# An adaLN block of gated linear attention and an FP4 feed-forward: modulation loads moved to other slots, and the last rows' down products in two column halves

## The chip, the cores and the metric

The kernel runs on one core of one Trainium2 chip. The metric is the device time of one execution in microseconds; the median of several runs is compared. The profile is one further execution, taken by the hardware profiler.

## What is computed

The input x has 2 batches of 4096 rows of 512. Six modulation rows per batch come from a small product. The first half of the block is a gated scan, the second a feed-forward whose operands are quantized blockwise to FP4 and back.

```python
mod = (_silu(L0_c) @ L0_wmod).reshape(2, 6, 1, -1)
sa, ca, ga, sb, cb, gb = (mod[:, i] for i in range(6))
ga, gb = (sign(g) * max(abs(g), 0.25) for g in (ga, gb))
h = layernorm(x) * (1 + ca) + sa
x = x + ga * attn(h)      # q, kv, a = rmsnorm(h) @ W; y = scan(sigmoid(a), kv); q * y
h = layernorm(x) * (1 + cb) + sb
x = x + gb * ffn(h)       # fp4(silu(fp4(h) @ wg) * (fp4(h) @ wu)) @ fp4(wd)
```

`ffn` has an inner width of 1408. Products that have to be nearly as exact as float32 are made as three passes over pairs of 16-bit parts (high x high, high x low, low x high); `PASSES` at line 419 lists them.

## The kernel before, in words

**Two stages.** The 8192 rows are 64 tiles of 128 rows (`NT`). Stage one makes the attention for 16 blocks of 512 rows (4 tiles each) and stores x plus the gated result to `out`. It also quantizes the feed-forward's weights on the side. Stage two takes the 64 tiles one after another through the feed-forward.

**Stage one, slots.** The loop at line 850 goes over slots 4 to 66 (the opening at line 717 holds slots 0 to 3 and the preparation of weights). Slot `i * 4 + e` makes the products of block `i` for output columns `e` of 128: `mix` (line 421), 3 parts (gate, value, query) x 4 chunks x 3 passes = 36 products of 128x512, each part in a PSUM bank; even and odd slots use different banks. Within the same slot stand the steps of other work, in a written order:

- tile `g = slot + 4` of the next block: `norm_hi` on ACT, `norm_lo` (line 403 on DVE, then `norm_turn`, line 409: the DMA transpose of this tile into the block's `xT`). The fourth of these transposes belongs to slot `4i + 3`, and the first product of slot `4i + 4` needs it.
- the previous slot's products: sigmoid (line 442), scan on DVE (448), read-out (459), a copy that splits halves (`yh`, 466), its DMA transpose `yt` (471); two slots on the joined copy (477), the residual add on POOL (485) and the store (490).
- moments and centring of the tiles after that; the load of x for tile `g + 3` (line 360).
- units of weight work: slots 5 to 21 load two weight pieces each for their maxima (`plan`), then come `collect`, `spread` and `finish` (lines 527 to 540: the maxima go through DRAM to all partitions), then one piece a slot is quantized, its transpose at line 553 or 576.

The whole stage stands in `tc.manual_schedule`, so each engine has the instructions of its queue in the order in which the Python code makes them. SP issues all loads and transposes in one queue; POOL issues the stores. In a slot SP has, in this order: the loads of the coming weight pieces (503 or 509), the load of x (360), the transpose `xT` (409), the transpose `yt` (471), the transpose of a quantized weight piece, and last the modulation loads.

**Modulations.** Rows 0 to 2 are made in the opening. Rows 3, 4 and 5 are made later: `load_mod` (line 224) brings `wmod` in quarters of 256 KB, one at the end of each of slots 5 to 16; `mod_rows` (line 238) makes the products after slot 19's own; at the end of slot 20 `mod_store` turns them to rows (lines 255 to 258 and 267) and POOL stores them to DRAM (line 270). `mod_load` (line 281, its issue in the profile at 283) loads one such row, spread over 128 partitions (256 KB): two of them at the end of slot 36 (`mods_for(0)`), and `mod_gb`, the gate of the feed-forward's output, at the end of slot 38.

```python
    MODS = 19
            rows = mod_rows(3, 4, 5) if slot == MODS else None
            if MODS - 14 <= slot < MODS - 2:
                m, k = divmod(slot - MODS + 14, KC)
                load_mod(3 + m, k, k + 1)
            if slot == NS // 2 + KC + 2:
                gbs[0] = mod_load(5, 0, "mod_gb")
```

**Stage two.** For each tile: `products` (line 947, 72 products), `silu`, `gated`, `quant_h`, and two tiles later `down` (line 994): 33 products of 128x512 into one PSUM tile (11 chunks x 3 passes). `finish` scales the result (line 1012) and adds it to `out` by an accumulating store from POOL (1018). The last tile is different: its x was loaded to `last_x1`, and `finish` scales, adds (1023) and stores (1024, on SP) two halves of 256 columns one after the other, both after the one sum of 33 products.

Of the kernel before, what the change touches and what calls it, by code (L numbers as in the profile page):

```python
# [8 lines left out]
F32 = mybir.dt.float32  # L9
# [4 lines left out]
ALU = mybir.AluOpType  # L14
# [4 lines left out]
P = 128  # L19
D = 512  # L20
KC = D // P
B = 2
N = 4096
# [8 lines left out]
NT = B * N // P  # L32
# [12 lines left out]
def tile_adaln_block(  # L45
# [13 lines left out]
    V, A, G, T, S = nc.vector, nc.scalar, nc.gpsimd, nc.tensor, nc.sync  # L59
# [16 lines left out]
    def side(shape):  # L76
        return pst.tile(list(shape), F32, name="sd", tag="sd")
# [18 lines left out]
    ring = None  # L96
# [318 lines left out]
    def new_xT():  # L415
        return apool.tile([P, 2 * KC, TB], F16, name="xT", tag="xT", bufs=2)
# [140 lines left out]
    def wd_chunk(wp, k):  # L557
        j = k * P // 512
        n0, n1 = CHUNKS[j]
        return 2 * (n0 // P) + wp * ((n1 - n0) // P) + k - n0 // P  # L560
# [34 lines left out]
    def load_units(items):  # L595
        got = []
        for kind, arg in items:
            if kind in ("max", "rows"):
                got.append((kind, arg, load_rows(arg[2], arg[0])))
            elif kind in ("maxd", "down"):  # L600
                got.append((kind, arg, load_down(*arg)))
            else:
                got.append((kind, arg, None))
        return got
# [7 lines left out]
    qx, x1s, xst, gbs = {}, {}, {}, {}  # L612
# [223 lines left out]
    def step(gen, n=1):  # L836
        for _ in range(n):
            if gen is not None:
                next(gen, None)
# [1 line left out]
    units, coming = [], []  # L841
    rows = None
    NS = NBLK * KC
    MODS = 19
    plan = [[]] * (KC + 1) + plan
    order = tc.manual_schedule(engines={V.engine, A.engine, G.engine, S.engine, T.engine})
    with order:
        xT, nxT = new_xT(), new_xT()
        gate, joining = opening(xT, nxT)
        for slot in range(KC, NS + 3):  # L850
            i, e = divmod(slot, KC)
            if e == 0 and slot < NS:
                xT = nxT
                nxT = new_xT() if i + 1 < NBLK else None
            units, coming = coming, load_units(plan[slot]) if slot < len(plan) else []
            g = slot + KC
            if g + 3 < NT:
                norm_load(g + 3)
            cur = None
            if slot < NS:  # L860
                got = []
                step(mix(i, xT, e, got), 3)
                cur = got[0]
            late = rows
            rows = mod_rows(3, 4, 5) if slot == MODS else None
            if slot == KC:
                gate = gates(*gate)
            if len(joining) == 2 or slot >= NS + 2:
                store(*residual(*joined(*joining.pop(0))))
            if g < NT:  # L870
                norm_hi(g)
            if gate is not None:
                gate = scan(*gate)
                carry_on(*gate)
            if g + 2 < NT:
                norm_moments(g + 2)
            if gate is not None:
                gate = read_out(*gate)
            if g < NT:
                norm_lo(g, nxT)  # L880
            if gate is not None:
                joining.append(turned(*halves(*gate)))
            if g + 2 < NT:
                norm_stats(g + 2)
            for u in units:
                u.advance(1)
            if g + 1 < NT:
                norm_center(g + 1)
            for u in units:
                u.advance(2)  # L890
                u.advance(3)
            if cur is not None:
                cur = gates(*cur)
            if g + 1 < NT:
                norm_shift(g + 1)
                norm_square(g + 1)
            for u in units:
                u.advance(4)
            coming = [Unit(*c_) for c_ in coming]
            for u in coming:  # L900
                u.advance(0)
            if g + 1 < NT:
                norm_gain(g + 1, G)
            for u in units:
                u.advance(5)
                u.advance(6)
            assert all(u.step == 7 for u in units)
            if MODS - 14 <= slot < MODS - 2:
                m, k = divmod(slot - MODS + 14, KC)
                load_mod(3 + m, k, k + 1)  # L910
            if late is not None:
                mod_store(*late)
            if slot == KC + 1:
                ca[1] = mod_load(1, 1, "mod_c1")
                sa[1] = mod_load(0, 1, "mod_s1")
            if slot == NS // 2 + KC:
                mods_for(0)
            if slot == NS // 2 + KC + 2:
                gbs[0] = mod_load(5, 0, "mod_gb")
            if slot in (NS - 6, NS - 5):  # L920
                for n in range(2):
                    n += 2 * (slot - NS + 6)
                    x1s[n] = load_x1(n)
            if NS - 5 <= slot < NS - 1:
                n = slot - NS + 5
                xst[n] = stats_x(x1s[n])
                if n in (1, 2):
                    run(quant_x(n - 1, x1s.pop(n - 1), xst.pop(n - 1)))
            gate = cur
    tc.no_sync_barrier()  # L930
    wgT, wuT, wdT = wts["wgT"], wts["wuT"], wts["wdT"]
# [3 lines left out]
    ring = ctx.enter_context(tc.tile_pool(name="ring", bufs=2))  # L935
# [49 lines left out]
        S.dma_start_transpose(hT, flat(hl))  # L985
        qh[i] = hT, u

    def down(i):
        hT, u = qh.pop(i)
        pd = side((P, D))  # L990
        n = 0
        for k in range(IC):
            for hp, wp in PASSES:
                T.matmul(  # L994
                    pd,
                    hT[:, hp * IC + k, :],
                    wdT[:, wd_chunk(wp, k), :],
                    start=n == 0,
                    stop=n == 3 * IC - 1,
                )  # L1000
                n += 1
        return i, pd, u

    def finish(i, pd, u):
        b, t0 = divmod(i * P, N)
        if b not in gbs:
            t = ring.tile([P, D], F32, name="mod_gb1", tag="mod_gb1", bufs=1)
            S.dma_start(t, modd[5][b : b + 1, :].to_broadcast([P, D]))
            gbs[b] = t
        o = ring.tile([P, D], F32, name="o", tag="o", bufs=3)  # L1010
        def scaled(d):
            V.scalar_tensor_tensor(  # L1012
                out=o[:, d], in0=pd[:, d], scalar=u, in1=gbs[b][:, d], op0=ALU.mult, op1=ALU.mult
            )

        if i < NT - 1:
            scaled(slice(0, D))
            G.dma_start(out[b, t0 : t0 + P, :], o, accum_op=ALU.add)  # L1018
            return
        for d0 in range(0, D, D // 2):  # L1020
            d = slice(d0, d0 + D // 2)
            scaled(d)
            V.tensor_tensor(o[:, d], o[:, d], last_x1[:, d], ALU.add)
            S.dma_start(out[b, t0 : t0 + P, d], o[:, d])

    LAG, LEAD = 2, 2
    qh = {}
# [4 lines left out]
    with tc.manual_schedule(engines={V.engine, A.engine, G.engine, S.engine, T.engine}):  # L1032
        h = None
        ended = []
        for i in range(NT):
            last = i == NT - 1
            work_i = products(i)
            downs = [] if i == NT - 2 else [i - LAG - 1, i - LAG] if last else [i - LAG]
            ending, ended = ended, [down(d) for d in downs if d >= 0]
            x = None  # L1040
            if i + LEAD < NT:
                x = quant_x(i + LEAD, x1s.pop(i + LEAD), xst.pop(i + LEAD))
            if i + LEAD + 2 < NT:
                x1s[i + LEAD + 2] = load_x1(i + LEAD + 2)
            step(x, 2)
            step(h)
            step(h)
            step(h, 2)
            sl = silu(0, *work_i)
            step(x)  # L1050
            if i + LEAD + 1 < NT and i > 0:
                xst[i + LEAD + 1] = stats_x(x1s[i + LEAD + 1])
            step(x)
            gated(0, sl, *work_i)
            step(x)
            sl = silu(1, *work_i)
            step(x)
            for e in ending:
                finish(*e)
            step(x, 4)  # L1060
            gated(1, sl, *work_i)
            gated(2, silu(2, *work_i), *work_i)
            h = quant_h(i, work_i[2])
            step(h, 3)
        step(h, 2)
        last_x1 = load_x1(NT - 1)
        finish(*ended.pop(0))
        step(h, 3)
        ended.append(down(NT - 2))
        finish(*ended.pop(0))  # L1070
        ended.append(down(NT - 1))
        for e in ended:
            finish(*e)


_TC = dict(schedule_with_timeline_sim=True)
# [45 lines left out]
```

## Time and profile before

| | |
|---|---|
| runs, median (lowest to highest) | 1910.6 us (1909.87 to 1911.59) |
| the profiled execution's own time | 1910.41 us |
| its span in the profile | 1908.3 us |
| granted TensorE clock | 0.999 |
| stage one / stage two, from the chain of waits | up to 534.3 us / after it |
| DMA share in 61.8 to 124.7, 124.7 to 187.0, 187.0 to 347.7 us | 0.93, 0.82, 0.80 |
| DMA share in 534.3 to 1875.0 us | 0.39 |
| SP's loads of `wmod`: count, median to landing | 24, 4.7 us |
| SP's `xT` and `yt` transposes: count, median to landing | 64 and 64, 3.5 and 3.2 us |

A row of the timeline has the start, the duration (of the whole group where several are merged), the engine, the line of the kernel, the operation, output<-input, the shape and the count; in brackets stands the idle time of that engine before it and what released it. PE is TensorE's products, PEld its weight loads, which run beside products. Ends of products are modelled, so a row's duration covers about 0.16 us more than the time to the next start. SPq rows are DMA issues: the duration is that of the issue, and the landing is told apart from it. The chain of waits follows the work that ended last back to what released each step.

### The profile page before, as it was taken

Reading aid. Unit: us, or ns where it says so; the run is one execution under the profiler, and the core shown is the slowest. Engines: PE = TensorE matmul, PEld = TensorE weight load, DVE = VectorE, ACT = ScalarE, POOL = GpSimd, SP = SyncE. Lnnn points to the kernel's source line nnn. Section 1 sums busy time; section 2 is a strip of 40 time slices with the busy share of each in tenths; the row PEclk is TensorE's granted clock in tenths of the full one; section 3 lists DMA queues with packets and bytes.
Section 4 is the critical chain, followed back from the end, with each engine's and each line's share of the span. In section 5 each row is a group of like instructions: output and inputs, shape, how many; then the busy total and the mean of one; then the engine's idle time right before and its main releaser. Section 6 shows DMA issues by size and latency. Waiting matters only on the chain.

```text
span 1908.3 us, 25838 instructions
## 1 busy us (share of the span) xinstructions
PE 1893.5 (99%) x9342; PEld 901.9 (47%) x9342; DVE 1603.3 (84%) x2670; ACT 999.1 (52%) x1702; POOL 407.7 (21%) x596
## 2 busy tenths in 40 slices
PE   8999999999999999999999999999999999999998
PEld 5444444444444444444444444444444444444444
DVE  7888799999869988888888888888888888888865
ACT  6555577777655544445444444445444544444432
POOL 5545566666421100000000000000000000000000
PEclk9999999999999999999999999999999999999999
DMA  6787679888533533433344334443344334433433
GB/s 222 196 240 214 155 197 201 218 199 202 134 86 64 96 64 68 80 75 64 64 79 80 64 64 86 77 74 67 69 80 75 64 64 80 80 64 64 70 62 59
DMA packets 469185, 203.26 MB, mean 107 GB/s; under 512 B 426247, under 2 KB 427527, under 8 KB 469057
## 3 DMA queue, kind: packets, MB, share of 16 engines
q1 hardware_dynamic: 454608, 168.09, 40.9%
q0 software_dynamic: 14448, 33.52, 9.1%
q8 instruction: 73, 1.20, 0.3%
q14 instruction: 56, 0.45, 0.1%
HBM read 62.86 MB, written 33.58 MB: 51 GB/s over the span
## 4 chain that ended last, share of the span: by engine, by line
PE 92%; DVE 4%; DMA 2%; ACT 1%; issue 1%; POOL 0%; SPq 0%; ACTq 0%; DVEq 0%
PE mm L947 47%; PE sd L994 24%; PE mm L430 20%; DVE ld L176 1%; PE sd L230 0%; DMA yt<-yh 0%; DMA xr<-in_L_attn_x_dram 0%; DVE hl L403 0%; DVE ld L170 0%; ACT y L477 0%; DVE y L448 0%; DMA xT<-hl 0%; DMA scratch<-in_L_wmod_dram 0%; DVE scratch L334 0%; DVE y L459 0%
## 5 line engine op out<-in xcount | busy, mean ns | idle before, releaser
L947 PEld LDWEIGHTS <-x2T 128*128 128x128 f16 x4608 | 450.9, 98 | 469.0 <-issue 0.8
L430 PE MATMUL mm<-xT,wqT 128*128 128x512 f16 (+1 forms) x2412 | 499.0, 370 | 3.2 <-ACT cy L454 1.6
L947 PE MATMUL mm<-wuT,x2T 128*128 128x512 f16 (+1 forms) x2304 | 487.7, 361 | 0.5 <-DVE hid L967 0.5
L947 PE MATMUL mm<-wgT,x2T 128*128 128x512 f16 (+1 forms) x2304 | 487.7, 361 | 0.0
L994 PE MATMUL sd<-wdT,hT 128*128 128x512 f16 x2112 | 465.8, 379 | 0.0
L430 PEld LDWEIGHTS <-wqT 128*128 128x128 f16 x2412 | 229.4, 98 | 271.7 <-issue 4.4
L994 PEld LDWEIGHTS <-hT 128*128 128x128 f16 x2112 | 206.6, 98 | 242.7
L962 ACT ACTIVATE silu<-mm,u 128x512 f32<-128x512 f32 (+1 forms) x192 | 124.7, 650 | 284.9 <-PE mm L947 281.1
L967 DVE SCALAR_TENSOR_TENSOR hid<-mm,u,silu 128x512 f32<-128x512 f32 (+1 forms) x192 | 128.6, 673 | 138.8 <-PE mm L947 130.2
L635 POOL TENSOR_SCALAR rstd<-vs 128x1 f32<-128x1 f32 x64 | 14.9, 232 | 989.1 <-ACT sq L633 989.1
L144 ACT ACTIVATE u<-ud,rms 128x1 f32<-128x1 f32 x64 | 18.9, 295 | 278.8 <-DVE rms L140 278.8
L121 ACT ACTIVATE sle<-sl 128x512 f16<-128x512 f32 (+2 forms) x162 | 146.9, 907 | 0.0
L114 ACT ACTIVATE she<-sh 128x1408 bf16<-128x1408 bf16 (+1 forms) x128 | 128.3, 1002 | 4.1
L1018 POOL DMA_DIRECT2D out_dram<-o x63 | 55.5, 881 | 271.4 <-DVE o L1012 267.6
L466 ACT COPY yh<-y 128x1024 uint16<-128x1024 uint16 x64 | 66.9, 1045 | 88.4 <-DVE y L459 80.5
L123 DVE SCALAR_TENSOR_TENSOR xn<-hid,xn 128x1408 f32<-128x1408 f32 x64 | 103.6, 1619 | 3.7 <-ACT hid L117 3.7
L107 DVE TENSOR_TENSOR xn<-hid,inv 128x1408 f32<-128x1408 f32 x64 | 104.0, 1625 | 2.2
L126 DVE SCALAR_TENSOR_TENSOR hhl<-hid,xn 128x1408 f16<-128x1408 f32 x64 | 104.0, 1625 | 2.2
L148 DVE TENSOR_REDUCE amh<-hid 128x88 f32<-128x1408 f32 x64 | 103.7, 1620 | 2.2
L117 ACT ACTIVATE hid<-xn 128x1408 f32<-128x1408 f32 x64 | 88.1, 1377 | 30.9 <-DVE xn L107 30.9
L123 DVE SCALAR_TENSOR_TENSOR xn<-ld,xn 128x512 f32<-128x512 f32 (+1 forms) x98 | 67.1, 684 | 29.5 <-ACT ld L117 29.3
L485 POOL TENSOR_TENSOR xr<-xr,y 128x512 f32<-128x512 f32 x64 | 81.9, 1279 | 18.7 <-ACT y L477 14.8
(129 smaller groups left out, 1913.2 us busy)
## 6 DMA issues: line engine op xcount, KB each, us to landing
ld<-out_dram SPq DMA_DIRECT2D x65, 256.0 KB, 2.9
xr<-in_L_attn_x_dram SPq DMA_DIRECT2D x64, 256.0 KB, 3.7
out_dram<-xr POOLq DMA_DIRECT2D x64, 256.0 KB, 3.7
out_dram<-o POOLq DMA_DIRECT2D x63, 256.0 KB, 3.9
scratch<-in_L_wmod_dram SPq DMA_DIRECT2D x24, 256.0 KB, 4.7
ld<-in_L_ffn_w_gate_dram SPq DMA_DIRECT2D x22, 256.0 KB, 3.4
ld<-in_L_ffn_w_up_dram SPq DMA_DIRECT2D x22, 256.0 KB, 3.7
ld<-in_L_ffn_w_down_dram SPq DMA_DIRECT2D x16, 256.0 KB, 3.3
```

The costliest lines, as they stand in the source:

```text
L107: V.tensor_tensor(blocks(xn), blocks(src), spread(inv, nb), ALU.mult)
L114: A.activation(blocks(she), spread(sh, nb), AF.Copy, scale=WPEAK)
L117: A.activation(a, xn, AF.Abs, scale=MAGIC)
L121: A.activation(blocks(sle), spread(sl, nb), AF.Copy, scale=WPEAK)
L123: V.scalar_tensor_tensor(out=xn, in0=a, scalar=FLOOR, in1=xn, op0=ALU.max, op1=ALU.add)
L126: V.scalar_tensor_tensor(out=nq, in0=a, scalar=FLOOR, in1=xn, op0=ALU.max, op1=ALU.subtract)
L148: V.tensor_reduce(am, src.rearrange("p (b k) -> p b k", k=QB), AX.X, ALU.max, apply_absolute_value=True)
L430: T.matmul(pp[:, t : t + width], wqT[e][:, wp, k, part, :], xT[:, xp * KC + k, t : t + width], start=n == 0, stop=n == 3 * KC - 1,)
L947: T.matmul(pp[:, : n1 - n0], x2T[:, xp * KC + k, :], wt[:, wp * KC + k, n0:n1], start=n == 0, stop=n == 3 * KC - 1,)
L962: A.activation(sl[:, :w], pairs[j][0][:, :w], AF.Silu, scale=u[:, 0:1])
L967: V.scalar_tensor_tensor(out=hid[:, n0:n1], in0=pairs[j][1][:, : n1 - n0], scalar=u[:, 1:2], in1=sl[:, : n1 - n0], op0=ALU.mult, op1=ALU.mult,
L994: T.matmul(pd, hT[:, hp * IC + k, :], wdT[:, wd_chunk(wp, k), :], start=n == 0, stop=n == 3 * IC - 1,)
```

## The change

The products of rows 3 to 5 move from slot 19 to slot 22. The twelve quarter loads keep their order but stand at the ends of those slots from 5 to 20 that aren't 6, 10, 14 or 18. `mod_gb`'s load moves from the end of slot 38 to the end of slot 40. The last tile's down products are made by `last_down`, as two sums of 33 products of 256 columns in two banks of `products`; each half is scaled, added and stored by itself. The order on the other engines is otherwise the same; in stage two, instructions differ in the last tile alone.

```diff
-    MODS = 19
+    MODS = 22
+    QUARTERS = [slot for slot in range(5, 21) if slot % KC != 2]
...
-            if MODS - 14 <= slot < MODS - 2:
-                m, k = divmod(slot - MODS + 14, KC)
+            if slot in QUARTERS:
+                m, k = divmod(QUARTERS.index(slot), KC)
                 load_mod(3 + m, k, k + 1)
...
-            if slot == NS // 2 + KC + 2:
+            if slot == NS // 2 + 2 * KC:
                 gbs[0] = mod_load(5, 0, "mod_gb")
...
+    def down_part(hT, pd, d):
...
-                    wdT[:, wd_chunk(wp, k), :],
+                    wdT[:, wd_chunk(wp, k), d],
...
+    def last_down(i):
+        hT, u = qh.pop(i)
+        b, t0 = divmod(i * P, N)
+        o = new_out()
+        for n in range(2):
+            d = slice(n * D // 2, (n + 1) * D // 2)
+            pd = bank(n)[:, : D // 2]
+            down_part(hT, pd, d)
+            scaled(o[:, d], pd, u, gbs[b][:, d])
+            V.tensor_tensor(o[:, d], o[:, d], last_x1[:, d], ALU.add)
+            S.dma_start(out[b, t0 : t0 + P, d], o[:, d])
...
         ended.append(down(NT - 2))
         finish(*ended.pop(0))
-        ended.append(down(NT - 1))
         for e in ended:
             finish(*e)
+        last_down(NT - 1)
```

More of the change, by code (lines that the diff above doesn't have):

```diff
@@ L986, in quant_h @@
         qh[i] = hT, u
-    def down(i):
-        hT, u = qh.pop(i)
-        pd = side((P, D))
+    def down_part(hT, pd, d):
         n = 0
@@ L1001, in down, with new_out, scaled @@
                 n += 1
+    def down(i):
+        hT, u = qh.pop(i)
+        pd = side((P, D))
+        down_part(hT, pd, slice(0, D))
         return i, pd, u
+    def last_down(i):
+        hT, u = qh.pop(i)
+        b, t0 = divmod(i * P, N)
[7 more added lines that the diff above has]
+            S.dma_start(out[b, t0 : t0 + P, d], o[:, d])
+    def new_out():
+        return ring.tile([P, D], F32, name="o", tag="o", bufs=3)
+    def scaled(o, pd, u, by):
+        V.scalar_tensor_tensor(out=o, in0=pd, scalar=u, in1=by, op0=ALU.mult, op1=ALU.mult)
     def finish(i, pd, u):
@@ L1009, in finish @@
             gbs[b] = t
[L1010 to L1024, printed above, removed]
+        o = new_out()
+        scaled(o, pd, u, gbs[b])
+        G.dma_start(out[b, t0 : t0 + P, :], o, accum_op=ALU.add)
     LAG, LEAD = 2, 2
```

## The prediction

> **What bounds the kernel now.** I read the busy shares first, then TensorE's waits, then the timeline at each wait, then the end. The shares leave little room:
>
> ```profile
> PE 1893.5 (99%) x9342; PEld 901.9 (47%) x9342; DVE 1603.3 (84%) x2670; ACT 999.1 (52%) x1702; POOL 407.7 (21%) x596
> ```
>
> The change removes no arithmetic, so it can only gain where PE stands still, or after PE's last product. The PE rows of the timeline name every stop after the opening (idle time and releaser in brackets; these are rows of three windows):
>
> ```profile
> 61.82 62.32 PE L430 MATMUL mm<-xT,wqT 128*128 128x512 f16 x288 [1.10 <-issue]
> 124.74 5.57 PE L430 MATMUL mm<-xT,wqT 128*128 128x512 f16 x25 [0.59 <-DMA xT<-hl]
> 347.67 12.68 PE L430 MATMUL mm<-xT,wqT 128*128 128x512 f16 x58 [1.55 <-ACT cy L454]
> ```
>
> A slot is 36 products (3 parts x 4 chunks x 3 passes). 288 products are 8 slots in 62.33 us in the chain of waits, so 7.78 us a slot and 216 ns a product. Counting slots from the end of the stage (864 products = 24 slots before 534.31), 347.67 is the start of slot 40, 124.74 of slot 12, 61.82 of slot 4. All three begin a block, whose first product needs the last of the four xT transposes of the slots before. The releaser of the third (a 0.2 us copy) is only the last event seen. The SP rows show the cause:
>
> ```profile
> 326.16 4.28 SPq L471 DMA_TRANSPOSE yt<-yh  x1
> ...
> 340.00 0.58 SPq L283 DMA_DIRECT2D mod<-modd  x1
> 340.63 1.44 SPq L503 DMA_DIRECT2D ld<-in_L_ffn_w_gate_dram  x1
> 342.12 0.46 SPq L360 DMA_DIRECT2D xr<-in_L_attn_x_dram  x1
> 342.69 1.75 SPq L409 DMA_TRANSPOSE xT<-hl  x1
> ```
>
> The xT issued at 342.69 lands 4.7 us later by its own view, at 347.39; PE goes at 347.67 and was free at 346.12. Two things made it late: two modulation loads at 322.23 (end of slot 36), behind which the yt transpose of 326.16 took 7.9 us to land and held the scan chain of slots 38 and 39, and the single load at 340.00, which stands in the queue right ahead of this xT.
>
> The end, from the last 132 down products on:
>
> ```profile
> 1874.84 28.65 PE L994 MATMUL sd<-wdT,hT 128*128 128x512 f16 x132
> ...
> 1903.53 0.49 DVE L1012 SCALAR_TENSOR_TENSOR o<-sd,u,mod_gb 128x256 f32<-128x256 f32 x1 [6.37 <-PE sd L994]
> 1904.05 0.42 DVE L1023 TENSOR_TENSOR o<-o,ld 128x256 f32<-128x256 f32 x1
> 1904.39 0.48 DVE L1012 SCALAR_TENSOR_TENSOR o<-sd,u,mod_gb 128x256 f32<-128x256 f32 x1
> 1904.50 1.20 SPq L1024 DMA_DIRECT2D out_dram<-o  x2
> 1904.90 0.42 DVE L1023 TENSOR_TENSOR o<-o,ld 128x256 f32<-128x256 f32 x1
> ```
>
> Both halves of the last rows wait for the whole sum; four DVE steps and two stores follow PE's end, and the second store, issued at 1905.36, lands 1.7 us later.
>
> **Part 1, the last down products in halves.** 33 products of 512 columns become 66 of 256, each with a weight load. The unknown is the pitch at 256 columns. The trace has both sides of it: 36 products of 128 columns take 2.18 us in the opening (27.49), start to start 56 ns with a 98 ns weight load each; 132 products of 512 take 28.50 us in the chain, 216 ns. On the line between them 256 columns cost 109 ns, so 66 cost 7.2 us against 7.1 now: +0.1. The Trainium skill speaks against it: "TensorE: Matmul & The Clock Gate", section "Back-to-back issue gap", says that in a stream of weight load and product pairs the spacing is set by both, and gives 81 ns at N=128 where the formula has 56. By that rule the weight load adds 25 ns to each, 66 x 25 = 1.7 us, and the split would lose. This trace has such a stream at 56, so I take +0.1, with bounds 0 and +1.7.
>
> What comes back: the first half's two DVE steps and its store (0.49 + 0.42 and the issue) now run beside the second half's 3.6 us of products. After PE's end only 0.48 + 0.42 remain, and the second store goes out about 0.86 us earlier (1905.36 less 1904.50, the place that the first store has now). SP's closing waits keep their order. Sum: -0.86 + 0.1 = -0.75. The accumulating store of the rows before, issued at 1897.45, is done by 1903.2 and stays hidden. The two product banks were read long before, so nothing waits for them.
>
> **Part 2, mod_gb's load from the end of slot 38 to the end of slot 40.** Its 256 KB leave the queue ahead of the critical xT. DVE has that tile ready at 341.03 + 0.74 = 341.77, so the transpose could be issued 0.8 us earlier; the 256 KB are also about 0.65 us of DMA at the 370 to 400 GB/s that this stretch reaches, and xT landed in 3.3 to 4.6 us elsewhere in these slots, not 4.7. Bounds: if only the DMA time is saved, 0.65; if issue and landing both improve (341.86 + 4.1 = 346.0), the whole 1.55. Nothing at all is possible if the gate load's 1.44 us issue has another cause. The two loads of slot 36 stay, so I take a middle value, -1.1. In its new place it stands ahead of slot 41's loads of a weight row and of x, and of xT(41), none of which PE waits for before slot 44. The xT that slot 44 needs lands at 372.72 + 4.6 = 377.3 against 378.8 and is issued some 18 us after the load. Cost there: 0, bounded by 1.5 less the slack, also about 0.
>
> **Part 3, the twelve 256 KB loads.** Each is one SP issue of 0.57 us. They stood at the ends of slots 5 to 16; three leave slots 6, 10 and 14, and three appear in 17, 19 and 20. Do the removed ones delay PE now? Only slot 12 stops (0.59). Its xT was issued at 118.88, when DVE had it ready; slot 10's load was issued at 113.67 and had landed after 3.2 us, at 116.9. So it isn't in the way. While PE waits, the DMA view of 122.5 to 123.7 shows an idle data queue and one instruction packet:
>
> ```profile
> q8 instruction: 1, 0.02, 4.9%
> q1 hardware_dynamic: 5, 0.00, 1.2%
> ```
>
> Its 16 KB hold one DMA engine, and the transpose with it. The change doesn't touch that: gain 0, at best 0.59. Slot 4's 1.10 lies before all of this. The added loads: slot 20 now begins right after slot 19 (the 3.54 us of modulation products no longer stand between), and its xT, issued at 181.78, lands at 184.9 against 187.0. The 2.1 us of slack hold one load's 0.65. The last load lands near 202, its products start near 210. Cost 0.
>
> **Part 4, the products three slots later.** The same 3.54 us on PE. Behind them go three ACT row steps, three DVE steps and three POOL issues, which now stand at the start of slot 24 and not of slot 21. At 193.3 to 198.4 they held DVE for 5.1 us (3.1 waiting for ACT, the rest work); queued behind are the scan and, on POOL, the residual and its store. At slot 24 the chain has more room: DVE waited 2.28 us ahead of the scan at 227.11. Next late is the spread of the weight maxima (POOL L531, issued 225.22, landed 230.2, read at 231.73), since it also waits for the row stores. It would land near 232 (DVE's norm step came 2.4 us after PE's start of slot 21 and 0.9 after that of slot 24, so about 1.5 us later), DVE waits some tenths, and the 1.25 us that it waits for PE at 234.88 swallow them. The xT for slot 28 has 2.5 us (246.69 + 3.6 against 252.8). I take 0; bounds 0 and +1.
>
> **Sum.** -0.75 - 1.1 = -1.85. A saved stop passes on whole, as PE has no wait but 0.55 us at 565.96, which is fed by PE's own products. The profiled execution took 1910.41 (span 1908.29 and 2.1 around it), 0.2 below the runs' median of 1910.6. From 1910.41 that is 1908.56, on the median's footing 1908.8. A measurement of this kernel can tell about 0.2% (3.8 us) from no change, so this is a gain inside "same".
>
> **Rivals.**
> - Only the end gains. The loads at slot 36 alone keep xT late, or slot 44 takes over the stop. For it: yt's 7.9 us landing came before mod_gb. Against: mod_gb and the gate load fill SP from 340.00 to 342.07. 1910.6 - 0.75 = 1909.9.
> - Everything at a block's start goes, slot 12 as well: -0.75 - 1.55 - 0.59 = -2.9, 1907.7. Against it is the instruction packet.
> - Slower: weight loads are not hidden at 256 columns. Place: the last 66 products. If load and product follow each other, the pitch is 98 + 107 = 205 ns, 13.5 us against 7.1: +6.4, with -0.86 and -1.1 this gives 1915.0. It decides against the change from a pitch of (1.96 / 66) + 108 = 138 ns on. The 56 ns stream speaks against it.
> - Part 4 or the new loads make a stop of their own at slot 20, 24 or 28 of 1 to 3 us: 1910 to 1912.
>
> **How the numbers follow.** Forecast 0.62 (1908.0 to 1909.4), end only 0.18, everything 0.08, unhidden weights 0.05, a new stop 0.07. Leaving out the unhidden weights and part of the new stops, the range is 1907.5 to 1910.7. Faster by over 0.2% needs under 1906.8, more than all stops together: 0.03. Slower by over 0.2% is above 1914.4: the unhidden weights and a large new stop, 0.06. Same: 0.91.
>
> **What would show it.** Part 1: 66 rows of 128x256 at about 109 ns, one DVE pair after PE's end, the last store issued about 1.0 us after PE's last product (now 1.85). Part 2: no L283 row between the wgT transpose and xT of slot 39, slot 40's idle time under 0.6 us. Part 3: slot 12 still stops by about 0.6. Part 4: no PE idle at slots 20, 24 and 28. Wrong if the idle time at slot 40 stays at 1.5, or if a stop appears where none is now.

## The result, and the profile after

| | before | after |
|---|---|---|
| median of 22 runs each (lowest to highest) | 1910.01 us (1907.68 to 1912.43) | 1907.28 us (1905.12 to 1910.27) |
| ratio after / before, 95% interval | | 0.9983 (0.9977 to 0.9990) |
| span of the profiled execution | 1908.3 us | 1907.2 us |
| slot 4's first product to stage two's first | 61.82 to 534.14: 472.32 us | 63.95 to 533.80: 469.85 us |
| last tile's first down product to the span's end | 12.08 us | 11.32 us |
| time of an execution outside its span, mean | 2.11 us (2.06 to 2.19) | 1.78 us (1.72 to 1.83) |

The ratio is worth 3.2 us (1.9 to 4.4), the two medians differ by 2.7. Both lie within the 0.2% that count as no change here, and 1907.28 lies 0.2 below the range that was forecast. The three runs that were shown at first had a median 0.6 above that of the 22, so the forecast gain of 1.85 would have given 1908.2 on this footing. The last row compares each run's time with its own span, from the first to the last instruction; on the left are the 129 executions of the kernel before that are listed beside the experiments, on the right the 22 of the changed one. About 0.34 us of the gain thus lies outside the span, where the forecast has no part; what makes it is open.

The changed kernel's page, busy shares and the chain that ended last:

```profile
PE 1895.6 (99%) x9375; PEld 907.1 (48%) x9375; DVE 1602.9 (84%) x2670; ACT 999.0 (52%) x1702; POOL 408.1 (21%) x596
...
PE 98%; DVE 1%; DMA 0%; POOL 0%; ACT 0%; issue 0%; SPq 0%; DVEq 0%
```

PE has 33 products more, as foreseen, and the chain hardly leaves PE. The changed kernel's timeline, PE rows:

```profile
63.95 147.79 PE L430 MATMUL mm<-xT,wqT 128*128 128x512 f16 x684 [0.66 <-issue]
211.67 3.61 PE L244 MATMUL sd<-scratch,sc 128*2 128x512 f32 x24
215.22 318.74 PE L430 MATMUL mm<-xT,wqT 128*128 128x512 f16 x1476
533.80 2.75 PE L948 MATMUL mm<-wgT,x2T 128*128 128x512 f16 x12
```

From slot 4 to stage two there is no idle time in brackets any more: neither slot 40 nor slot 12 stops, nor do slots 20, 24 and 28. The two stops of before were shown as 0.59 and 1.55 us, 2.14 together; the stage is 2.47 shorter. The idle column starts to count at a modelled end, which lies about 0.16 us behind the time at which the next product could have started, so each stop cost some 0.15 more than shown: 0.75 and 1.7.

The changed kernel's SP rows around the xT of slot 39, which slot 40 needs:

```profile
339.19 1.23 SPq L553 DMA_TRANSPOSE wgT<-hl  x1
340.47 0.57 SPq L503 DMA_DIRECT2D ld<-in_L_ffn_w_gate_dram  x1
341.09 0.42 SPq L360 DMA_DIRECT2D xr<-in_L_attn_x_dram  x1
342.31 1.37 SPq L409 DMA_TRANSPOSE xT<-hl  x1
```

No modulation load (L283) stands in front; the weight load's issue takes 0.57 us where it took 1.44. Counted from slot 4's first product the transpose is issued 2.5 us earlier (278.36 against 280.87) and lands after 4.5 us. Of these 2.5 us, 1.65 are there already at the weight transpose ahead of them (275.24 against 276.89): about 0.75 is slot 12's stop, the rest comes from the yt transpose behind the two loads of slot 36. Its view in the changed kernel:

```profile
  ACT yh L466: 3.1, 1
...
DMA to landing us min/median/max: 7.0/7.0/7.0
```

Before, it landed after 7.9 us and ACT waited 4.0 for it.

The changed kernel's end:

```profile
1895.88 7.37 PE L993 MATMUL mm<-wdT,hT 128*128 128x256 f16 x66
...
1900.65 3.94 SPq L1019 DMA_DIRECT2D out_dram<-o  x2
1903.29 0.48 DVE L1025 SCALAR_TENSOR_TENSOR o<-mm,u,mod_gb 128x256 f32<-128x256 f32 x1 [2.66 <-PE mm L993]
1903.80 0.42 DVE L1018 TENSOR_TENSOR o<-o,ld 128x256 f32<-128x256 f32 x1
```

(7.37 - 0.16) / 66 is 109 ns a product: no weight load shows. One DVE pair stands after PE, and the two stores, merged in the L1019 row, end their issue at 1904.6. End to end 0.76 us are gone.

So the forecast's first part came in almost exactly, slot 40 gave more than forecast, and slot 12 gave something where nothing was expected. In this pair of profiles 2.47 + 0.76 = 3.2 us. That this is also the size of the ratio is chance: without the 0.34 outside the span, the runs gained 2.9 inside it by the ratio and 2.4 by the medians. The two profiled spans differ by only 1.1, because the opening of this one execution was 2.13 us longer (slot 4 at 63.95, not 61.82); that is taken up at the end.

### The profile page after: what moved, and what is told of

It is laid out like the page before. It is cut to its first block, busy times and chain, and to the rows that moved or that the text cites. A ratio compares the mean times of both kernels' runs of the same rounds, so it can differ in the third digit from the quotient of the medians.

```text
span 1907.2 us, 25896 instructions
## 1 busy us (share of the span) xinstructions
PE 1895.6 (99%) x9375; PEld 907.1 (48%) x9375; DVE 1602.9 (84%) x2670; ACT 999.0 (52%) x1702; POOL 408.1 (21%) x596
## 4 chain that ended last, share of the span: by engine, by line
PE 98%; DVE 1%; DMA 0%; POOL 0%; ACT 0%; issue 0%; SPq 0%; DVEq 0%
PE mm L948 47%; PE mm L430 26%; PE sd L993 24%; PE sd L230 1%; PE mm L993 0%; DMA xr<-in_L_attn_x_dram 0%; PE sd L244 0%; DVE hid L968 0%; POOL rn L392 0%; DVE hhl L126 0%; DVE amh L148 0%; DVE xn L107 0%; ACT scratch L295 0%; DVE xn L123 0%; POOL ss L390 0%
## 5 line engine op out<-in xcount | busy, mean ns | idle before, releaser
L993 PE MATMUL sd<-wdT,hT 128*128 128x512 f16 x2079 | 458.7, 379 | 0.0
```

The lines of the kernel that those rows point to most:

```text
L993: T.matmul(pd, hT[:, hp * IC + k, :], wdT[:, wd_chunk(wp, k), d], start=n == 0, stop=n == 3 * IC - 1,)
```

## The experiments

Eleven kernels, each profiled once and timed in 10 to 20 executions of its own beside the kernel before on the same chip. "b" kernels start from the kernel before, "a" kernels from the changed one. Two questions were open: which of the three edits brings what, and why slot 12 stops or doesn't. For the second there were two theories: that one load less ahead of the xT of slot 11 moves this transpose against the instruction packet; and that it is the load of slot 10 itself, the last before it. All results stand in one table; times in it are us. "Stage" is slot 4's first product to stage two's first, "packet" the start of PE's instruction packet, counted from slot 4's first product, "xT(11)" the time from issue to landing of the transpose that slot 12 needs.

| kernel | ratio (95%) | stage | stop at 12 | stop at 40 | packet | xT(11) | slot 4 at |
|---|---|---|---|---|---|---|---|
| before | | 472.32 | 0.59 | 1.55 | 60.8 | 5.8 | 61.82 |
| b_again, unchanged | 0.9998 (0.9989 to 1.0006) | 475.92 | 0.75 | 2.88 | 61.4 | 5.8 | 60.84 |
| b_gb40 | 0.9996 (0.9988 to 1.0005) | 471.00 | 0.31 | 0.45 | 60.6 | 5.3 | 63.89 |
| b_quarters | 0.9994 (0.9986 to 1.0003) | 471.84 | none | 1.84 | 63.0 | 3.2 | 60.80 |
| b_halves | 0.9997 (0.9989 to 1.0006) | 471.28 | none | 1.28 | 60.5 | 3.2 | 63.74 |
| b_pair40 | 0.9996 (0.9986 to 1.0006) | 471.06 | none | 1.06 | 60.4 | 3.2 | 62.15 |
| b_gb3 | 1.0024 (1.0017 to 1.0031) | 476.68 | 0.51 | 4.65 | 60.8 | 5.8 | 60.66 |
| b_no10 | 0.9997 (0.9987 to 1.0008) | 474.88 | none | 3.07 | 62.4 | 3.2 | 64.15 |
| b_no6 | 0.9996 (0.9986 to 1.0007) | 471.41 | none | 1.41 | 63.6 | 3.2 | 61.97 |
| after | 0.9983 (0.9977 to 0.9990) | 469.85 | none | none | 62.8 | 3.2 | 63.95 |
| a_with10 | 0.9984 (0.9976 to 0.9991) | 469.85 | none | none | 62.3 | 3.2 | 60.53 |
| a_again, unchanged | 0.9985 (0.9978 to 0.9991) | 470.13 | none | none | 63.0 | 3.2 | 60.47 |
| a_384 | 0.9979 (0.9970 to 0.9987) | 469.84 | none | none | 64.0 | 3.2 | 61.83 |

b_again also had a stop of 0.26 at slot 8.

### The kernel before again, and each part alone

**b_again** is the kernel before, unchanged.

> The kernel before once more, unchanged, for a second profile. Theory A (slot 12's stop comes from an instruction packet that happens to hit its xT in that one execution): slot 12 may start without a stop this time; slot 40's stop of about 1.5 us is there again, since it follows from the order of the queue. Theory B (the load at slot 10 makes slot 12's stop): both stops again, about 0.6 and 1.5 us idle. Time: ratio 1.000 +- 0.001. From slot 4's first product to stage two's first product: 472.3 us with both stops, 471.6 with slot 40's alone.

Its stop at slot 40 is 2.88 us, almost twice that of the first profile, and something follows it. The kernel before again, the PE row of the timeline, and then the table of stretches around the stop, whose columns are PE's, PEld's, DVE's, ACT's and POOL's busy time, PE's granted clock, DMA share and GB/s:

```profile
348.60 188.33 PE L430 MATMUL mm<-xT,wqT 128*128 128x512 f16 x864 [2.88 <-DMA xT<-hl]
```

```profile
348.60:350.60 2.00, 2.00 (x7) 0.76 (x8) 2.00 (x5) 1.37 (x2) 1.20 (x3) 0.64 1.02 226
350.60:352.60 2.00, 2.00 (x6) 0.74 (x5) 1.91 (x4) 1.24 (x3) 0.58 (x1) 0.50 0.82 289
352.60:354.60 2.00, 2.00 (x11) 0.88 (x9) 1.16 (x4) 1.53 (x5) 0.14 (x1) 1.00 1.24 243
```

The 864 products take 188.33 us here and 186.64 in b_gb40, b_pair40 and others: 1.7 us more, because the granted clock is one half for 3.4 us. Here the stop costs 2.88 + 0.15 + 1.7 = 4.7 us. So what part 2 can remove differs from one execution to the next.

**b_gb40** moves only `mod_gb`'s load.

```diff
-            if slot == NS // 2 + KC + 2:
+            if slot == NS // 2 + 2 * KC:
```

> Before, with mod_gb's load at the end of slot 40 and nothing else changed. My step (part 2) said 1.1 us of the 1.55 go. The profile of the changed kernel lets expect all of it: no stop at slot 40, -1.7 us. Rival (the moved quarters made the room that the changed kernel has at slot 40): the stop stays at over 1 us, less than -0.5 us. Slot 12: stop as in the kernel before, by chance (A) or always (B).

The stop at slot 40 falls to 0.45, and slot 12 keeps its stop. That is 1.1 less than in the first profile of the kernel before. In b_gb40 the yt transpose behind the two loads of slot 36, by its own view:

```profile
  ACT yh L466: 4.0, 1
...
DMA to landing us min/median/max: 7.9/7.9/7.9
```

ACT waited 4.0 us for it, as long as in the kernel before. The changed kernel, with the same pair of loads, issues the xT of slot 39 2.1 us earlier after slot 4 (278.36 against 280.43). About 0.5 of that is slot 12's stop and about 0.9 the yt transpose. In the five kernels with the products at slot 22 (b_quarters and the four changed ones) it lands after 6.1 to 7.0 us, in the seven that have them at slot 19 and the pair at slot 36 after 7.7 to 8.0. Moving the twelve loads and the products therefore helps slot 40 too; by what path is open. The rest stands in b_gb40's SP rows:

```profile
341.87 0.58 SPq L503 DMA_DIRECT2D ld<-in_L_ffn_w_gate_dram  x1
342.50 1.72 SPq L360 DMA_DIRECT2D xr<-in_L_attn_x_dram  x1
344.32 1.23 SPq L409 DMA_TRANSPOSE xT<-hl  x1
```

Here it is the load of x whose issue is long, and no modulation load is near. So the weight load's 1.44 us in the kernel before need not be the doing of `mod_gb`'s load. An instruction packet of 16 KB starts at 342.36 in b_gb40 and at 340.46 in the kernel before, just ahead of the long issue in both. In the kernel before and all "b" kernels but b_pair40, some load (of `mod_gb`, a weight, x, or b_gb3's spare one) has an issue of 1.3 to 2.0 us that starts within 0.2 us of this packet. In b_pair40 the packet comes later, and the loads there issue in 0.42 to 0.57 us, `mod_gb`'s included. That the packet makes an issue long is a reading from this coincidence; no run moved the packet alone.

**b_quarters** moves only the twelve quarter loads and the products to slot 22 (`MODS = 22` and the `QUARTERS` lines of the change).

> Before, with the quarter loads in the new slots and the products in slot 22, nothing else. My step: 0 us. Theory B: slot 12's stop is gone, -0.8 us, in every profile; theory A: slot 12 stops or not as it does in the kernel before, and the time is the same. Both: slot 40's stop of 1.5 us stays, no stop at slots 20, 24 and 28.

Slot 12's stop is gone, slot 40's stays (1.84), and no stop comes at 20, 24 or 28. In its two stages up to the last tile b_quarters differs from the changed kernel by `mod_gb`'s place alone. With the load at slot 38 the xT of slot 39 is issued at 279.10 us after slot 4 and lands after 5.9; in the four changed kernels it is issued at 277.6 to 278.4 and lands after 4.5 to 5.8. The stage is 2.0 us longer (471.84 against 469.85), which is the stop of 1.84 and the 0.15 that its column leaves out. This is the plainest measure of part 2, though b_quarters has one profile only. **b_halves** makes only the last tile's down products in halves (`down_part`, `last_down` and the call, as in the change).

> Before, with the last down products in two halves and nothing else. My step: from the last tile's first down product to the span's end 0.75 us less (66 products at 109 ns, one pair of DVE steps and one store after PE's end). Rival of unhidden weights: over 1 us more. The stops at slots 12 and 40 as in the kernel before. Time -0.75 us, too small for the ratio to show alone.

Its end takes 1897.11 to 1908.415 = 11.31 us, as in the changed kernel. Slot 12 doesn't stop although stage one is that of the kernel before: here the transpose of slot 11 was issued 56.6 us after slot 4's first product, not 57.0 or later, and was through before the packet of 60.5.

None of the three parts can be told from no change by its ratio alone: intervals are 0.0017 wide, a part is worth 0.0004 to 0.001. It is the stops in the profiles that place the gains. By the ratios the three sum to 1.3 thousandths of 1910, 2.5 us, with an uncertainty of about that size. Of b_quarters' 1.1 us some 0.35 lie outside the span: it and b_no10 have 1.76 us there, as the changed kernels have, and the other six built on the kernel before have 2.1.

### The load ahead of slot 39's transpose, undone and multiplied

**b_pair40** leaves `mod_gb`'s load where it was and moves the other two, of slot 36, to slot 40.

```diff
-            if slot == NS // 2 + KC:
+            if slot == NS // 2 + 2 * KC:
                 mods_for(0)
```

> Before, with the pair of loads of slot 36 moved to the end of slot 40; mod_gb stays at slot 38. If the pair's late yt is the larger cause of slot 40's stop: no stop at slot 40, xT of slot 39 issued some 3 us earlier than in the kernel before (near 277.8 us after slot 4's first product, not 280.9), and a new, smaller stop at slot 44 at most (0 to 0.8 us). If mod_gb alone makes the stop, slot 40 stops by over 1 us as before.

Its SP and PE rows:

```profile
337.32 0.57 SPq L283 DMA_DIRECT2D mod<-modd  x1
...
339.48 1.51 SPq L409 DMA_TRANSPOSE xT<-hl  x1
```

```profile
346.73 186.64 PE L430 MATMUL mm<-xT,wqT 128*128 128x512 f16 x864 [1.06 <-issue]
```

The transpose is issued early, at 277.33 us after slot 4 (before: 280.87), and still slot 40 stops, because it lands only after 7.2 us (3.8 in b_gb40). So slot 40 can stop without the pair. But this run doesn't show how much of the landing is the single load's doing: an instruction packet starts at 343.21, in the middle of this transfer, and in the trace packets of the transpose then take up to 2.4 us each, as in the transfer that slot 12 waits for. Against b_halves, which has no stop at slot 12 either and issues this transpose at 279.90, it is issued 2.6 us earlier, so the pair does hold it back. The moved pair makes no stop at slot 44.

**b_gb3** issues `mod_gb`'s load three times at slot 38; the two added ones bring the same 256 KB to a buffer that nothing reads.

```diff
             if slot == NS // 2 + KC + 2:
                 gbs[0] = mod_load(5, 0, "mod_gb")
+                for n in range(2):
+                    S.dma_start(piece(2, n, 1), modd[5][0:1, :].to_broadcast([P, D]))
```

> Before, with mod_gb's 256 KB loaded three times at the end of slot 38 (two of them to memory that nothing reads). If each load in front of xT of slot 39 costs its DMA time of 0.65 us, slot 40's stop grows from 1.3 to 1.8 us idle to 2.6 to 3.2, and [...]the granted clock halves for 3.4 us after it, as in the second profile of the kernel before, so that 1.7 us more are lost: from slot 4's first product to stage two's 475 to 476 us. If the load only took the place of an idle queue, the stop stays at 1.3 to 1.8.

The only kernel whose interval lies wholly above 1. Its PE row:

```profile
349.52 187.98 PE L430 MATMUL mm<-xT,wqT 128*128 128x512 f16 x864 [4.65 <-DMA xT<-hl]
```

The stop grows to 4.65 us and the half clock comes too; it begins 0.7 us before PE goes on, so it costs 1.3 us (187.98 against 186.64). By ratio it costs 4.6 us more than the kernel before (1.0024 x 1910.1). Two loads more add 1.8 to 3.1 us to the stop of the kernel before (2.88 and 1.55), so 0.9 to 1.5 for each. Loads in front of the transpose lengthen slot 40's stop: with the load behind it is 0.45 (b_gb40) or none, with three in front it is longer than in any other profile. The stop's scatter with one load in front, 1.06 to 3.07, is not explained by the load.

### Slot 12

**b_no10** takes the load out of slot 10 alone; the twelve loads then stand in slots 5 to 17. **a_with10** is the changed kernel with a load in slot 10 and none in slot 20. **b_no6** takes it out of slot 6 alone.

```diff
b_no10  +    QUARTERS = [slot for slot in range(5, 18) if slot != 10]
a_with10+    QUARTERS = [slot for slot in range(5, 20) if slot not in (6, 14, 18)]
b_no6   +    QUARTERS = [slot for slot in range(5, 18) if slot != 6]
```

> Before, with the quarter load of slot 10 taken out (the later ones move by one slot, the last stands in slot 17). Theory A (an instruction packet, some 60.5 to 63 us after slot 4's first product, that hits xT or misses it): it may hit or miss, and its time decides: near 61 it hits and xT of slot 11 lands in over 5 us, near 63 it misses and xT lands in 3.2 us. Theory B (slot 10's load itself): xT of slot 11 lands in 3.2 us. B also says that the packet comes later, near 63, as in the two kernels with the new slots, if the packet is what the load shifts.

> The changed kernel with a quarter load in slot 10 again (and none in slot 20). Theory B: xT of slot 11 lands in over 5 us again and slot 12 stops by 0.3 to 0.8 us; the packet comes near 61. Theory A: as chance has it, by the packet's time alone. Slot 40: no stop in either.

> Before, with the quarter load of slot 6 taken out (later ones move by one slot, the last stands in slot 17). If any one load less ahead of slot 11 moves the packet: it comes at 62.3 to 63 us, xT of slot 11 lands in 3.2 us, slot 12 doesn't stop. If slot 10's load alone did that in the kernel without it: the packet comes near 61 and slot 12 may stop. Slot 40 stops by 1.3 to 3 us as in the kernels before.

All three are without a stop at slot 12. That the load of slot 10 is to blame falls with a_with10, which has it, and with b_no6, which has it too: one load less ahead of slot 11 goes with it, whichever of the two tried. One profile without a stop would prove little, since b_halves and b_pair40 have none with all the loads in place; the packet's time tells more. What differs is the moment at which PE's instruction packet (16 KB) meets the transpose. The landing of xT(11) in the DMA views of the kernel before, from 116 us on, and of the changed one, from 118:

```profile
xT<-hl SPq DMA_TRANSPOSE x1, 5.8
```

```profile
xT<-hl SPq DMA_TRANSPOSE x1, 3.2
```

Each of the two stretches holds one packet of the instruction queue. In the kernel before it comes at 122.7 us, while the transpose of 118.88 is under way; in the changed one at 126.8, when the transpose of 121.0 has landed at 124.2. In the table: where all of slots 5 to 10 have a load, the packet comes at 60.4 to 61.4 us and the transpose is late in four kernels of six; with one or more of these loads less it comes at 62.3 to 64.0 and the transpose is late in none of seven.

What the DMA engines moved in the kernel before, in GB/s for each quarter of a us from 116 us on:

```profile
GB/s 385 393 410 410 410 442 361 377 328 148 0 0 0 0 98 295 377 314 242 290 292 194 207 254 49 0 66 0 0 0 5 9 10 119 293 386 393 369 393 393
```

The 66 is the packet, at 122.67. The transfer stands still from 122.2 and goes on at 123.6, when the packet is through. It thus stops half a us before the packet's recorded start, and at its usual 3.2 us it would have landed at 122.1. So that the fetch holds the transpose is a reading from what comes together, and the margin is thin. In the table's terms the usual landing would be at 60.3 and the packet is at 60.8; in b_pair40 the landing is at 59.9 and the packet at 60.4, and there the transpose is not late. Why one load of 256 KB less puts the packet off by about 2 us is open; no run asked for that.

### The changed kernel again, and a faster end

**a_again** is the changed kernel, unchanged.

> The changed kernel once more, for a second profile. If its gain is that of its own order and not of one lucky execution: 469.9 us from slot 4's first product to stage two's, no stop at slot 12 or 40, the packet at 62.3 us or later. If the stops come and go by chance: one of them is there. Time: ratio 0.998 +- 0.001 again.

No stop at slots 12 and 40 again, and its end takes 11.32 us; the last tile's down products waited 0.28 us for a transpose, which the first profile doesn't have. **a_384** splits the last rows in 384 and 128 columns, so that less is left after the last product. The 81 ns in its expectation are the page's figure that part 1 weighed.

```diff
-        for n in range(2):
-            d = slice(n * D // 2, (n + 1) * D // 2)
-            pd = bank(n)[:, : D // 2]
+        for n, d in enumerate((slice(0, 384), slice(384, D))):
+            pd = bank(n)[:, : d.stop - d.start]
```

> The changed kernel with the last down products in parts of 384 and 128 columns. By the pitches seen: 33 x 162 ns + 33 x 56 ns = 7.2 us, as now; after PE's end one pair of DVE steps of 128 columns, about 0.6 us where 256 columns take 0.9. Theory of hidden weights: from PE's first part to the span's end 0.3 us less than in the changed kernel. By the rule of 81 ns at 128 columns: 33 x 25 ns = 0.8 us more on PE, so 0.5 us longer. Time: same within 0.1%.

The end of a_384:

```profile
1893.75 7.37 PE L993 MATMUL mm<-wdT,hT 128*128 128x384 f16 x66
...
1901.16 0.35 DVE L1024 SCALAR_TENSOR_TENSOR o<-mm,u,mod_gb 128x128 f32<-128x128 f32 x1 [0.63 <-PE mm L993]
1901.54 0.29 DVE L1017 TENSOR_TENSOR o<-o,ld 128x128 f32<-128x128 f32 x1
```

The row merges both widths under the first one's name. 33 products of 384 and 33 of 128 columns take the same 7.2 us as 66 of 256, so weight loads stay hidden at 128 columns too. 0.35 + 0.29 us of DVE follow PE instead of 0.48 + 0.42, and what follows DVE, the store above all, takes 2.79 us instead of 2.97. The end is 1893.75 to 1904.62 = 10.87 us, 0.45 less; 0.3 had been expected. This is the fastest kernel measured, 1906.36 us (12 runs, beside 1910.24 before), though its interval overlaps with that of a_again.

## Why the prediction was right or wrong

The sign was right, and the gain stayed under 0.2% as forecast, but the time came out 1.5 us under 1908.8 and 0.2 under the range. Three terms make up the 1.5. The median of three runs from which the forecast started was 0.6 above that of 22: luck. The "2.1 around" the span was carried over as fixed; in the changed kernel it is 1.8, and no part of the forecast has these 0.34 us. The remaining 0.5 were gained inside the span (2.4 by the medians, where -1.85 was forecast). In the first pair of profiles that last term is larger, 1.4. There the step that failed is part 3, and with it the middle value of part 2. By the stops, the case that came true is the rival in which everything at a block's start goes (-2.9).

**Part 1, forecast -0.75, measured -0.76.** Every term held: 109 ns a product, one DVE pair after PE, the first half beside the second. b_halves alone shows it too. The rule that the prediction weighed (the Trainium skill, "TensorE: Matmul & The Clock Gate", section "Back-to-back issue gap", 81 ns at 128 columns) does not hold here: a_384 shows the 128-column products at the pitch of the line (56 ns) once more.

**Part 2, forecast -1.1, measured about -1.7 in the first profile.** That the load in front makes slot 40's stop longer was right; b_quarters against the changed kernel shows it with 2.0 us. Moved alone, in b_gb40, it took 1.1 off the stop, which is the forecast, though the scatter of the stop is larger than that. The term that was mis-sized in the whole change is the "middle value" between 0.65 and 1.55, taken because "the two loads of slot 36 stay". They stayed, but with the quarter loads and products moved they held yt 0.9 us less, and slot 39 no longer inherited the 0.75 of slot 12's stop, so the issue became earlier by 2.5 us and not by 0.8. The gate load's long issue, which the prediction laid to `mod_gb` with a doubt, goes with the instruction packet in the traces and not with the load. Two things lie beyond the upper bound. A stop costs some 0.15 more than its idle column. And the forecast took the stop of one execution for that of all: the six profiles with both places of loads unchanged show 1.55, 2.88, 1.84, 1.28, 3.07 and 1.41 (before, b_again, b_quarters, b_halves, b_no10, b_no6), and two of these paid 1.7 us more to the clock.

**Part 3, forecast 0, measured about -0.75 in the first profile.** This step failed: "Its 16 KB hold one DMA engine, and the transpose with it. The change doesn't touch that: gain 0, at best 0.59." The change does touch it. The loads of slots 5 to 10 bear on when the packet comes, and with one of them less it comes some 2 us later and the transpose lands after 3.2 us in seven kernels of seven. In two of the six kernels with the old places slot 12 didn't stop either, so the gain is not 0.75 in every execution. The same move also gave slot 40 the 0.9 us named under part 2.

**Part 4, forecast 0, measured 0.** No idle time of PE at slots 20, 24 and 28 in any kernel with the products at slot 22.

**Sum.** 0.76 + 1.7 + 0.75 = 3.2 in one pair of profiles. The runs gained 2.4 to 2.9 inside the span and 0.34 outside it. The half clock has little share in that: the mean of the granted clocks on record is 0.9985 for 129 executions before and 0.9986 for 60 of the changed kernel, its repetition and a_with10, about 0.2 us apart. Not settled: what changes the time outside the span, why the pair at slot 36 holds yt less after the move, and what moves the packet.

## What to carry to other kernels

A transpose that the next block waits for should have no load right ahead of it in its queue: here one of 256 KB cost the stage 2.0 us (one profile of b_quarters against four without it). A stall seen in one profile is one draw; take a second profile before sizing what its removal can bring, since here the same stop was 1.3 to 3.1 us long and the longer ones cost another 1.7 us of half clock. When a fetch that no line of the kernel issues is in the way, ask what moves it, before calling it out of reach. And compare a run's time with its span: a part of a small gain can lie outside everything that the profile shows.

## What the runs showed of the hardware that was not expected

**A stop of three microseconds can halve the clock.** Stops of 2.88, 3.07 and 4.65 us each came with 3.4 us at a granted clock of one half; those of 1.84 us and less with none, and none between was met. The Trainium skill ("TensorE: Matmul & The Clock Gate", section "HAM oscillation — how this bites in real kernels") warns of idle gaps above some 3.4 us; here 2.88 + 0.15 = 3.0 us was enough. That the half-clock stretch lasts 3.4 us agrees with the window of 3413 ns that the section "What's actually happening" states. In these traces the changes of the clock stand whole multiples of 3.413 us apart: in b_again it rises at 4.43 us and falls at 349.18, 101 windows later. The window before that fall held 0.6 us of PE's work, the one in b_no10 0.8, the one in b_gb3 none, while b_quarters' stop of 1.84 us left each window over 2. So a window need not be wholly idle, and it may matter how a stop lies to the windows; no run tried that.

**The opening decides much of an execution's scatter.** Profiles of the changed kernel, its first one and then a_again, same columns as above:

```profile
10.00:20.00 10.00, 10.00 (x25) 4.22 (x24) 6.96 (x12) 3.01 (x5) 2.75 (x7) 0.73 1.04 405
30.00:40.00 10.00, 10.00 (x156) 9.59 (x155) 8.10 (x21) 7.47 (x16) 8.04 (x14) 0.88 0.79 250
```

```profile
10.00:20.00 10.00, 8.75 (x61) 4.79 (x62) 9.70 (x17) 6.21 (x12) 3.48 (x9) 1.00 1.05 405
30.00:40.00 10.00, 10.00 (x121) 7.46 (x118) 8.56 (x21) 7.38 (x16) 7.28 (x13) 1.00 0.58 211
```

With the clock at 0.73 and 0.88 in these stretches slot 4 begins at 63.95 us, with the full clock at 60.47. Over the 13 profiles it begins at 60.5 to 60.8 where the opening has no half-clock window of 3.4 us, at 61.8 to 62.2 with one and at 63.7 to 64.2 with two or three. That is a spread of 3.7 us, where 22 runs of the changed kernel spread over 5.2 (1905.12 to 1910.27). Executions with the same mean clock compare better: at 0.999 the median is 1909.8 us in 17 runs before and 1906.9 in 12 of a_again, 2.9 apart.
